# Attention of the first image: value products in four column tiles, softmax sums on VectorE

## The chip, the cores and the metric

The kernel runs on one core of one Trainium2 chip. A core has five engines with queues of their own: TensorE (PE in the profile, its weight loads PEld), VectorE (DVE), ScalarE (ACT), GpSimd (POOL) and the engine SP, which here only starts DMAs. SBUF is the working memory and PSUM the memory that TensorE writes its products to. Each has 128 partitions, and PSUM has eight banks of 512 float32 columns. All data here is float32. The metric is the time of one launch on the device in microseconds (us), lower is better.

## The reference, cut to what matters

The program is four layers on a tensor of 4 images with 384 channels and 64 x 64 positions. The change touches the attention of layer 0 alone, which for one image (batch index b) computes, with N = 4096 positions:

```python
q, k, v = qkv[:, :16], qkv[:, 16:32], qkv[:, 32:]       # 16, 16 and 96 channels, N positions
attn = softmax(einsum('bcn,bcm->bnm', q, k) * 0.25, axis=-1)
out  = einsum('bcn,bmn->bcm', v, attn)                   # 96 channels, N positions
xm   = relu(concatenate([out, x_skip], axis=1))          # 384 channels again
y    = bn(einsum('oc,bchw->bohw', w_proj, xm))
x    = x + y
```

Each output position is a mean of the 96-channel values over all 4096 positions, weighted by exponentials of scores and divided by the sum of these exponentials. The other three layers (a Fourier filter with a 3 x 3 convolution and a gate, a large block with two depthwise convolutions, a 7 x 7 convolution) come after it and are not touched.

## The kernel before, in words

`phase_a` runs layer 0 and layer 1. Its loop over the four images pairs two streams of work in `side_by_side`: `attention(b, ...)`, and `others(b, ...)`, which is the input statistics (`x_norm`) and the queries, keys and values (`qkv`) of image b+1 and layer 1 of image b-1. For b = 0 there is no earlier image, so `others` has only `x_norm(1)` and `qkv(1)`. `side_by_side` takes pieces of `others` at an even pace over the 64 steps of the attention.

A step of `attention` is a pair (i, c): query block i of 512 positions, and key chunk c of 512 positions, eight of each. Three things belong to a step:

- Scores (`scores`, L772): four matmuls, one to each quarter of 32 partitions of the array, each with 32 rows of contraction (16 channels and padding). They fill the four-bank PSUM tile `sc_s`, of which there is one (`p4`, bufs=1). Keys lie on the partitions of the result, queries on its columns.
- Exponentials (L780): ScalarE reads `sc_s` in two halves of 1024 columns and writes the SBUF tile `probs`, 2048 columns, of which there are two.
- Values times probabilities (L809): four matmuls of 128 keys each, N = 512, accumulated over the 32 matmuls of a query block into one PSUM bank `av`. The stationary operand `vt[:, 4c+v, :]` has 128 columns: 96 value channels, and 32 columns of ones. Partitions 96 to 127 of `av` therefore end up with 32 copies of the softmax sum.

A float32 matmul appears in the trace as two passes, each with a weight load of its own. So a step has 8 passes of scores and 8 passes of values.

The scores of step n+1 are written ahead of the values of step n in the program, and under `tc.high_priority()`. The Tile framework turns the program into one fixed queue for each engine before the launch: it takes instructions by priority (earlier in the program first, unless raised) as its model finds them ready, and places the semaphore waits. Each queue then runs in order on the chip.

When a query block is complete, `finish` inverts the sums (L792, 32 x 512 on VectorE) and writes `xm` as max(av, 0) times the inverse in three pieces of 32 partitions (L795). `layer0_end` follows over the next steps: it loads the input block `x_res`, normalises the other 288 channels (L831, L835), multiplies by the projection (L842: three groups of three matmuls, `proj_m`), adds the residual (L849), takes statistics (L621) and stores the block to `xa` from GpSimd's queue (L852).

PSUM in this phase: four banks for `sc_s`, two banks with the tag "a" (`pa`, `av` takes one for a query block, so one is always spare), two banks with the tag "m" (`pm`), which all other products share: `proj_m`, `ln_s`, `ln_v`, `qk_m`, `v_m`.

Of the kernel before, what the change touches and what calls it, by code (L numbers as in the profile page):

```python
# [9 lines left out]

# [1 line left out]

# [1 line left out]

# [5 lines left out]
F32 = mybir.dt.float32  # L22
AF = mybir.ActivationFunctionType
ALU = mybir.AluOpType
# [4 lines left out]
NJ = 3  # L29
P = 128  # L30
PD = 96
# [7 lines left out]
TAPS = (2, 2, 2, 2, 2, 2, 4, 4)  # L39

UNITS = C // 32

_CONST_COLS = {}
_VEC_COLS = {}
# [230 lines left out]
class _Builder:  # L275
    def __init__(self, ctx, tc, ins, out):
# [16 lines left out]

        self.tok = self.dram.tile([UNITS, B, 32, N], F32, tag="tok", name="tok")

# [13 lines left out]
        self.d53 = [  # L309
            [self.dram.tile([32, B, 32, P], F32, tag=f"d{i}{u}", name=f"d_{i}_{u}") for u in range(UNITS)]  # L310
            for i in range(2)
# [128 lines left out]
    def qkv_weights(self, pool):  # L440

        nc = self.nc
        w = self.wk("wq_raw", "lx", 2)[:, 0:PD]
        nc.scalar.dma_start(w, self.ins["w_qkv"])
        inv, shift = self.bn_scale_shift(
            "bn1", self.vec("bn1_m"), self.vec("bn1_v"), self.vec("bn1_g"), self.vec("bn1_b")
        )
        nc.vector.tensor_scalar(w, w, inv, None, ALU.mult)  # L450
        pt = self.pm("wq_pt")
        nc.tensor.transpose(pt[0:PD, 0:P], w, self.ident)
        wt = self.wk("wq_t", "ln", 3)[0 : PD + 1, 0:P]
        raw = self.wk("wq_rawt", "lx", 2)[0:PD, 0:P]
        nc.vector.tensor_copy(raw, pt[0:PD, 0:P])
        nc.vector.tensor_scalar(wt[0:PD, :], raw, self.vec("ln_w", PD), None, ALU.mult)
        pb = self.pm("wq_pb")
        nc.tensor.matmul(pb[0:1, 0:P], lhsT=self.vec("ln_b", PD), rhs=raw, start=True, stop=False)
        nc.tensor.matmul(pb[0:1, 0:P], lhsT=shift, rhs=self.ident, start=False, stop=True)
        nc.scalar.copy(wt[PD : PD + 1, :], pb[0:1, 0:P])  # L460

        self.wq4 = pool.tile([PD + 1, 4, 32], F32, tag="wq4", name="wq4")
        self.wk4 = pool.tile([PD + 1, 4, 32], F32, tag="wk4", name="wk4")
        self.wv = pool.tile([PD + 1, P], F32, tag="wv", name="wv")
        for t in (self.wq4, self.wk4, self.wv):
            nc.gpsimd.memset(t, 0.0)
        nc.gpsimd.memset(self.wk4[PD : PD + 1, :, 0:1], 1.0)
        nc.gpsimd.memset(self.wv[PD : PD + 1, PD:], 1.0)
        for g in range(4):
            nc.vector.tensor_copy(self.wq4[:, g, 1:17], wt[:, 0:16])  # L470
            nc.vector.tensor_copy(self.wk4[:, g, 1:17], wt[:, 16:32])
        nc.vector.tensor_copy(self.wv[:, 0:PD], wt[:, 32:P])
        self.wqk = pool.tile([PD + 1, 4, 32], F32, tag="wqk", name="wqk")
        nc.vector.tensor_copy(self.wqk[:, 0:3], self.wq4[:, 0:3])
        nc.vector.tensor_copy(self.wqk[:, 3], self.wk4[:, 3])
        self.score_bound(pool, wt)
# [283 lines left out]
    def attention(self, b, q, k4, vt):  # L760

        tc, nc = self.tc, self.nc

        def scores(i, c):
            p = self.probs.tile([P, 2048], F32, tag="p", name="probs")
            s = self.p4("sc_s")

            with tc.high_priority():  # L770
                for g in range(4):
                    nc.tensor.matmul(  # L772
                        s[:, g],
                        lhsT=k4[32 * g : 32 * g + 32, c],
                        rhs=q[i][32 * g : 32 * g + 32],
                        start=True,
                        stop=True,
                    )
            for h in range(2):
                nc.scalar.activation(  # L780
                    p[:, h * 1024 : (h + 1) * 1024],
                    s[:, 2 * h : 2 * h + 2].rearrange("p a b -> p (a b)"),
                    AF.Exp,
                    scale=0.25,
                )
            return p

        def finish(av):

            xm = self.work.tile([P, NJ, 512], F32, tag="xm", name="xm", bufs=1)  # L790
            rd = self.wk("av_rd", "rd", 1)
            nc.vector.reciprocal(rd[PD:P], av[PD:P])  # L792
            for g in range(3):
                at = slice(32 * g, 32 * g + 32)
                nc.vector.scalar_tensor_tensor(xm[at, 0], av[at], 0.0, rd[PD:P], ALU.max, ALU.mult)  # L795
            return xm

        st = self.stats_tile("xa_st")
        steps = [(i, c) for i in range(8) for c in range(8)]
        ahead = scores(*steps[0])  # L800
        done, end = None, iter(())
        for n_step, (i, c) in enumerate(steps):
            p = ahead
            if n_step + 1 < len(steps):
                ahead = scores(*steps[n_step + 1])
            if c == 0:
                av = self.pa("av")
            for v in range(4):
                nc.tensor.matmul(  # L809
                    av,  # L810
                    lhsT=vt[:, 4 * c + v, :],
                    rhs=p[:, v * 512 : (v + 1) * 512],
                    start=c == 0 and v == 0,
                    stop=c == 7 and v == 3,
                )
            next(end, None)
            if c == 1 and done is not None:
                end = self.layer0_end(b, i - 1, finish(done), st)
            if c == 7:
                done = av  # L820
            yield
        for _ in self.layer0_end(b, 7, finish(done), st):
            pass
        self.norm1 = self.norm_of_stats(st)

# [220 lines left out]
    def phase_b(self):  # L1046
# [5 lines left out]
        with ExitStack() as ctx:  # L1052
# [17 lines left out]
            self.units(cp)  # L1070
            self.unit_x = [[] for _ in range(UNITS)]
            for u in range(UNITS):
                st = self.bt_p.tile([P, 2, 16, 6], F32, tag="st", name="st")
                strips = self.unit_strips(u + 1) if u + 1 < UNITS else iter(())
                tok = self.unit_tok(u - 1) if u else self.unit_strips(0)
# [8 lines left out]
                self.conv_norms(u, st)  # L1084
            for _ in self.unit_tok(UNITS - 1):
                pass
# [856 lines left out]
```

## Time and profile before

| | |
|---|---|
| median of three runs | 4893.77 us (4886.19 to 4898.56) |
| the profiled execution | 4883.64 us, of which the span from first to last instruction is 4881.8 us |
| instructions | 47092 |
| TensorE busy over the span | 4432.2 us (91%) |
| VectorE busy over the span | 2764.1 us (57%) |
| ScalarE busy over the span | 1988.4 us (41%) |
| GpSimd busy over the span | 728.7 us (15%) |
| attention of image 0 | from about 62 us to 495 us of the span |

The profile is of one execution. A group line names the source line, the engine, the operation, what is written and read, the shapes, the count, busy time and mean time of one instruction, and the idle time of the engine ahead of it with what ended it. The ends of matmuls are modelled, so the distance from one start to the next says more of the pace than a matmul's own duration does.

### The profile page before, as it was taken

To read this page: it belongs to the slowest core of one execution; us is meant where nothing else is said; L and a number is where in the kernel's file an instruction comes from. 1 tells how busy PE (TensorE), PEld (TensorE's weight loads), DVE (VectorE), ACT (ScalarE), POOL (GpSimd) and SP (SyncE) were. 2 spreads that over 40 slices of the span, in tenths; PEclk is the share of its full clock that TensorE was granted. 3 is DMA by queue.
4 is the path that set the end of the run, shared out by engine and by line. 5 is a ranking of instruction groups with operands and counts; after the bars stand their busy time and mean duration, and the time that the engine had idled before them with its cause. 6 is when DMAs were issued, how large, how long until landed. Compare 5 with 4: busy or idle time off the path is not lost. (4 is left out here: it accounts for less than half of the span.)

```text
span 4881.8 us, 47092 instructions
## 1 busy us (share of the span) xinstructions
PE 4432.2 (91%) x17289; PEld 2492.5 (51%) x17289; DVE 2764.1 (57%) x4506; ACT 1988.4 (41%) x2958; POOL 728.7 (15%) x593
## 2 busy tenths in 40 slices
PE   5999999999999999989978889699999997778888
PEld 2334444344443444435467878344444443667888
DVE  6322566655566455566867778555521113667898
ACT  3444344444444443436345556311133334753321
POOL 1000000000000000000034445000000001225544
PEclk9999999999999999999979999899999998788999
DMA  5211212121211111113259999766664444896776
GB/s 186 74 34 38 83 65 72 46 76 35 69 61 60 54 46 58 59 56 121 75 167 300 281 281 305 269 252 254 242 244 155 155 155 155 312 342 188 229 254 231
DMA packets 345844, 749.06 MB, mean 153 GB/s; under 512 B 22683, under 2 KB 172294, under 8 KB 336646
## 3 DMA queue, kind: packets, MB, share of 16 engines
q1 hardware_dynamic: 279864, 471.92, 31.3%
q0 software_dynamic: 32640, 151.28, 8.0%
q10 hardware_dynamic: 33102, 122.77, 6.5%
q8 instruction: 140, 2.29, 0.2%
q14 instruction: 98, 0.80, 0.1%
HBM read 443.62 MB, written 302.25 MB: 153 GB/s over the span
## 5 line engine op out<-in xcount | busy, mean ns | idle before, releaser
L809 PE MATMUL av<-probs,vt 128*128 128x512 f32 x2048 | 955.9, 603 | 0.0
L780 ACT ACTIVATE probs<-sc_s 128x1024 f32<-128x1024 f32 x512 | 497.8, 1020 | 785.4 <-PE av L809 784.7
L809 PEld LDWEIGHTS av<-probs,vt 128*128 128x128 f32 x2048 | 368.0, 191 | 468.3 <-issue 464.6
L1005 DVE SCALAR_TENSOR_TENSOR acc<-band,vecs,acc 128x512 f32<-128x512 f32 x708 | 496.5, 747 | 45.2 <-POOL band L966 40.0
L1499 PE MATMUL h_m<-f_h,cm_w_t 128*128 128x512 f32 x1152 | 497.2, 595 | 7.4 <-ACT f_h L1487 7.4
L1216 PE MATMUL conv_m<-toep,z 128*128 128x192 f32 (+1 forms) x2304 | 447.7, 356 | 17.7 <-DVE toep L1197 17.6
L1216 PEld LDWEIGHTS conv_m<-toep,z 128*128 128x128 f32 x2304 | 411.1, 198 | 40.7 <-issue 10.2
L1813 PE MATMUL conv_m<-toep,z 128*128 128x128 f32 x3072 | 395.3, 287 | 38.3 <-POOL toep L1800 19.8
L1813 PEld LDWEIGHTS conv_m<-toep,z 128*128 128x128 f32 x3072 | 380.7, 203 | 40.5 <-POOL toep L1800 20.2
L1445 PE MATMUL h_s<-e_tok,cm_w_t 128*128 128x512 f32 x768 | 363.0, 595 | 4.2 <-DVE e_tok L1430 4.2
L1499 PEld LDWEIGHTS h_m<-f_h,cm_w_t 128*128 128x128 f32 x1152 | 219.7, 191 | 284.9 <-issue 274.3
L1197 POOL TENSOR_TENSOR toep<-w,band 128x1280 f32<-128x1280 f32 x94 | 272.3, 2901 | 314.3 <-PE conv_m L1216 199.9
L1507 DVE BATCH_NORM_STATS2 h_st<-f_h 128x6 f32<-128x512 f32 x96 | 66.5, 694 | 429.6 <-ACT f_h L1506 429.6
L772 PE MATMUL sc_s<-q,k 32*128 32x512 f32 x2048 | 294.9, 645 | 10.6 <-ACT probs L780 10.1
L928 PE MATMUL t_m<-w_in_t,xb 128*128 128x384 f32 x768 | 278.4, 497 | 3.1 <-DVE coef L945 2.9
L842 PE MATMUL proj_m<-xm,w_proj_t 128*128 128x512 f32 x576 | 271.2, 610 | 6.8 <-DVE xm L795 6.8
L1452 ACT COPY e_h<-h_s 128x1024 f32<-128x1024 f32 x96 | 97.2, 1012 | 399.9 <-PE h_s L1445 399.9
L849 DVE SCALAR_TENSOR_TENSOR x_res<-proj_m,bn_c,x_res 128x512 f32<-128x512 f32 x96 | 71.9, 749 | 324.6 <-PE proj_m L842 324.4
L1445 PEld LDWEIGHTS h_s<-e_tok,cm_w_t 128*128 128x128 f32 x768 | 146.6, 191 | 188.6 <-issue 183.3
L1454 DVE BATCH_NORM_STATS2 h_st<-e_h 128x6 f32<-128x512 f32 x192 | 123.4, 685 | 206.6 <-ACT e_h L1452 206.5
L928 PEld LDWEIGHTS t_m<-w_in_t,xb 128*128 128x128 f32 x768 | 142.5, 191 | 140.2 <-issue 59.8
L1445 PE MATMUL h_s<-z,cm_w_t 128*128 128x512 f32 x384 | 196.0, 592 | 0.0
(390 smaller groups left out, 5974.1 us busy)
## 6 DMA issues: line engine op xcount, KB each, us to landing
d<-d_o ACTq DMA_DIRECT2D x96, 512.0 KB
c_d<-d SPq DMA_DIRECT2D x96, 512.0 KB
hid<-e_h ACTq DMA_DIRECT2D x16, 3072.0 KB
f_h<-hid SPq DMA_DIRECT2D x16, 3072.0 KB
x_in<-in_x SPq DMA_DIRECT2D x96, 256.0 KB
x_res<-in_x SPq DMA_DIRECT2D x32, 768.0 KB
xa<-x_res POOLq DMA_DIRECT2D x32, 768.0 KB, 3.9
xa_in<-xa SPq DMA_DIRECT2D x32, 768.0 KB
```

The lines of the kernel that those rows point to most:

```text
L772: nc.tensor.matmul(s[:, g], lhsT=k4[32 * g : 32 * g + 32, c], rhs=q[i][32 * g : 32 * g + 32], start=True, stop=True,)
L780: nc.scalar.activation(p[:, h * 1024 : (h + 1) * 1024], s[:, 2 * h : 2 * h + 2].rearrange("p a b -> p (a b)"), AF.Exp, scale=0.25,)
L809: nc.tensor.matmul(av, lhsT=vt[:, 4 * c + v, :], rhs=p[:, v * 512 : (v + 1) * 512], start=c == 0 and v == 0, stop=c == 7 and v == 3,)
L842: nc.tensor.matmul(m, lhsT=self.w_proj[:, j, o * P : (o + 1) * P], rhs=xm[:, j], start=j == 0, stop=j == NJ - 1,)
L928: nc.tensor.matmul(m[:, 0:C], lhsT=xb[:, j], rhs=self.w_in[:, j, :], start=j == 0, stop=j == NJ - 1,)
L1005: nc.vector.scalar_tensor_tensor(out, src(j, k), w, done, ALU.mult, ALU.add)
L1197: eng.tensor_tensor(t, self.w53[:, at : at + 160].rearrange("p (m n) -> p m n", n=8).unsqueeze(2).to_broadcast([P, 20, 8, 8]), band.rearra ...
L1216: nc.tensor.matmul(m[:, c * 256 + to : c * 256 + to + 64 * (k1 - k0)], lhsT=self.z_[:, at : at + P], rhs=t[:, 10 * c + k0 : 10 * c + k1].r ...
L1445: nc.tensor.matmul(s[:, v, :], lhsT=w1[:, j, o * P : (o + 1) * P], rhs=t[j][:, v * 512 : (v + 1) * 512], start=j == 0, stop=j == NJ - 1,)
L1454: nc.vector.bn_stats(st[:, o, 8 * b + 2 * i + v, :], h[:, o, v * 512 : (v + 1) * 512])
L1499: nc.tensor.matmul(m, lhsT=w2[:, o, j * P : (j + 1) * P], rhs=h[:, o, v * 512 : (v + 1) * 512], start=o == 0, stop=o == 5,)
L1813: nc.tensor.matmul(m[:, ch * P : (ch + 1) * P], lhsT=self.z_[:, at : at + P], rhs=t[:, 8 * c + 2 * i : 8 * c + 2 * i + 2].rearrange("p m a ...
```

## The change

For image 0 alone:

- The 96 value channels are taken as three slices of 32 columns. A step's products are then twelve matmuls (three slices of channels, four key subchunks) of 128 rows and 32 columns each. The table `PLAN` puts them in three rounds of four; in a round each of the four matmuls goes to a column tile of its own (quarter g of the array's columns, which is also partitions 32g to 32g+31 of the result). There are two accumulators, `av_0` and `av_1`: an entry (k, s, v) of the plan adds slice s with subchunk v into accumulator k. The two accumulators together hold 192 of 256 partition rows, and slices 0, 1 and 2 are each split over two places.
- The ones columns are not used there. `add_up` adds the probabilities of a query block on VectorE into `acc`, 1024 columns: one addition of the two halves of `probs` at c = 0, two additions at each other c, and a last one that folds 1024 columns to 512 at c = 7.
- `evacuate` copies the two accumulators out of PSUM with two copies on ScalarE and two on VectorE, at high priority. Both banks of the tag "a" are in use in a query block, so the next block's first products wait for these copies.
- `invert`: four matmuls with a 128 x 32 tile of ones, one to each column tile, sum `acc` over the partitions and lay the 512 sums out as 128 x 128 (32 copies of 128 positions in each quarter). One reciprocal of 128 x 128 follows.
- `finish_tiles`: four matmuls with a broadcast column of the identity spread the inverse back to 96 x 512, one addition joins the two copies, and one instruction makes `xm`.
- `scores` has no raised priority there.

For the other three images the instructions are those of before.

```diff
+PLAN = (
+    ((0, 0, 3), (0, 1, 2), (0, 2, 1), (0, 0, 0)),
+    ((1, 1, 0), (0, 1, 3), (0, 2, 2), (0, 0, 1)),
+    ((1, 1, 1), (1, 2, 0), (0, 2, 3), (0, 0, 2)),
+)
...
+        self.ones = pool.tile([P, 32], F32, tag="ones", name="ones")
+        nc.gpsimd.memset(self.ones, 1.0)
...
-            with tc.high_priority():
+            with tc.high_priority() if b else nullcontext():
...
+        def products(av, c, p):
+
+            quarter = lambda g: slice(32 * g, 32 * g + 32)
+            for n, jobs in enumerate(PLAN):
+                for g, (k, s, v) in enumerate(jobs):
+                    others = [x[g] for x in PLAN[:n]], [x[g] for x in PLAN[n + 1 :]]
+                    before, behind = (any(x[:2] == (k, s) for x in o) for o in others)
+                    nc.tensor.matmul(
+                        av[k][quarter(g)],
+                        lhsT=vt[:, 4 * c + v, quarter(s)],
+                        rhs=p[:, v * 512 : (v + 1) * 512],
+                        start=c == 0 and not before,
+                        stop=c == 7 and not behind,
+                    )
+
+        def add_up(c, p):
+
+            lo, hi = p[:, 0:1024], p[:, 1024:2048]
+            if c == 0:
+                t = self.blk.tile([P, NJ, 512], F32, tag="x", name="acc_p", bufs=1)
+                self.acc = t[:, 0:2].rearrange("p a n -> p (a n)")
+                nc.vector.tensor_add(self.acc, lo, hi)
+            else:
+                nc.vector.tensor_add(self.acc, self.acc, lo)
+                nc.vector.tensor_add(self.acc, self.acc, hi)
+            if c == 7:
+                self.prob_sum = self.wk("sum_p", "acc", 5)
+                nc.vector.tensor_add(self.prob_sum, self.acc[:, 0:512], self.acc[:, 512:1024])
+
+        def evacuate(av):
+
+            a, t = self.wk("av_a", "acc", 5), self.wk("av_t", "acc", 5)
+            with tc.high_priority():
+                nc.scalar.copy(t[0:32], av[0][96:128])
+                nc.vector.tensor_copy(a[0:PD], av[0][0:PD])
+                nc.scalar.copy(t[32:64], av[1][0:32])
+                nc.vector.tensor_copy(t[64:96], av[1][32:64])
+            return a, t
+
+        def invert(total):
+
+            m = self.pm("sum_m")
+            for g in range(4):
+                nc.tensor.matmul(
+                    m[32 * g : 32 * g + 32, 0:P],
+                    lhsT=self.ones,
+                    rhs=total[:, g * P : (g + 1) * P],
+                    start=True,
+                    stop=True,
+                )
+            rd = self.sm([P, P], "av_rd")
+            nc.vector.reciprocal(rd, m[:, 0:P])
+            return rd
+
+        def finish_tiles(a, t, rd):
+
+            xm = self.work.tile([P, NJ, 512], F32, tag="xm", name="xm", bufs=1)
+            m = self.pm("rd_m")
+            for g in range(4):
+                nc.tensor.matmul(
+                    m[0:PD, g * P : (g + 1) * P],
+                    lhsT=self.ident[:, 32 * g : 32 * g + 1].to_broadcast([P, PD]),
+                    rhs=rd,
+                    start=True,
+                    stop=True,
+                )
+            nc.vector.tensor_add(t[0:PD], t[0:PD], a[0:PD])
+            nc.vector.scalar_tensor_tensor(xm[0:PD, 0], t[0:PD], 0.0, m[0:PD], ALU.max, ALU.mult)
+            return xm
...
+        close = finish if b else finish_tiles
         for n_step, (i, c) in enumerate(steps):
             p = ahead
             if n_step + 1 < len(steps):
                 ahead = scores(*steps[n_step + 1])
...
+            if b == 0:
+                if c == 0:
+                    av = self.pa("av_0"), self.pa("av_1")
+                products(av, c, p)
+                add_up(c, p)
+                if c == 0 and done is not None:
+                    done = *done, invert(self.prob_sum)
+                if c == 7:
+                    evacuated = evacuate(av)
...
             if c == 1 and done is not None:
-                end = self.layer0_end(b, i - 1, finish(done), st)
+                end = self.layer0_end(b, i - 1, close(*done), st)
...
+        if b == 0:
+            done = *done, invert(self.prob_sum)
+        for _ in self.layer0_end(b, 7, close(*done), st):
             pass
```

More of the change, by code (lines that the diff above doesn't have):

```diff
@@ L13 @@
-from contextlib import ExitStack
+from contextlib import ExitStack, nullcontext
 import numpy as np
@@ L805, in attention @@
                 ahead = scores(*steps[n_step + 1])
[L806 to L815, printed above, removed]
+            if b == 0:
[7 more added lines that the diff above has]
+                    evacuated = evacuate(av)
+            else:
+                if c == 0:
+                    av = (self.pa("av"),)
+                for v in range(4):
+                    nc.tensor.matmul(
+                        av[0],
+                        lhsT=vt[:, 4 * c + v, :],
+                        rhs=p[:, v * 512 : (v + 1) * 512],
+                        start=c == 0 and v == 0,
+                        stop=c == 7 and v == 3,
+                    )
+                evacuated = av
             next(end, None)
             if c == 1 and done is not None:
-                end = self.layer0_end(b, i - 1, finish(done), st)
+                end = self.layer0_end(b, i - 1, close(*done), st)
             if c == 7:
-                done = av
+                done = evacuated
             yield
-        for _ in self.layer0_end(b, 7, finish(done), st):
+        if b == 0:
+            done = *done, invert(self.prob_sum)
+        for _ in self.layer0_end(b, 7, close(*done), st):
             pass
```

## The prediction

> **What bounds the kernel now.** First the busy table of the stretch that the change touches, and of its inside without the start (columns: length; busy us of PE, PEld, DVE, ACT, POOL; clock; DMA).
>
> ```profile
> core 0: us, PE busy (x) PEld busy (x) DVE busy (x) ACT busy (x) POOL busy (x), PEclk, DMA share, GB/s
> 62.00:495.00 433.00, 421.84 (x1383) 169.21 (x1381) 154.42 (x245) 183.60 (x223) 11.74 (x20) 0.98 0.20 62
> 124.00:488.00 364.00, 361.81 (x1194) 143.26 (x1192) 106.56 (x157) 154.86 (x183) 8.11 (x13) 1.00 0.15 48
> ```
>
> TensorE has no holes (361.8 of 364 us), VectorE is free 71% of the time, ScalarE 57%. Matmul ends are modelled, so I went to the timeline of one plain step to see whether TensorE is full or only waiting inside.
>
> ```profile
> 201.53 1.02 ACT L780 ACTIVATE probs<-sc_s 128x1024 f32<-128x1024 f32 x1
> 202.07 1.02 PE L809 MATMUL av<-probs,vt 128*128 128x512 f32 x2
> 203.02 0.31 PEld L772 LDWEIGHTS sc_s<-q,k 32*128 32x128 f32 x8 [0.76 <-ACT probs L780]
> 203.02 1.14 PE L772 MATMUL sc_s<-q,k 32*128 32x512 f32 x8
> ...
> 204.09 3.70 PE L809 MATMUL av<-probs,vt 128*128 128x512 f32 x8
> ...
> 205.06 0.19 PEld L809 LDWEIGHTS av<-probs,vt 128*128 128x128 f32 x1 [0.24 <-issue]
> 205.31 1.94 ACT L780 ACTIVATE probs<-sc_s 128x1024 f32<-128x1024 f32 x2 [2.76 <-PE av L809]
> 205.48 0.19 PEld L809 LDWEIGHTS av<-probs,vt 128*128 128x128 f32 x1 [0.24 <-issue]
> ...
> 207.72 0.31 PEld L772 LDWEIGHTS sc_s<-q,k 32*128 32x128 f32 x8 [0.76 <-ACT probs L780]
> ```
>
> A step lasts 4.70 us (203.02 to 207.72). Passes of values follow at 0.43 us (205.06, 205.48). Eight make 3.43 of the 3.63 us from 204.09 to 207.72; scores take 1.07, two passes deep, 0.86. So each change between the four-row tiling and the full array costs 0.20 us. The exponentials end at 207.25, 0.47 us ahead of the next scores: the "ACT probs" wait is only the last semaphore. 3.43 + 0.86 + 2 x 0.20 = 4.70: TensorE's own passes set the step.
>
> Last the groups of 124 to 488 us on VectorE, and from the page the price of its longest plain addition:
>
> ```profile
> L792 DVE RECIPROCAL av_rd<-av 32x512 f32<-32x512 f32 x7 | 23.5, 3363 | 36.5 <-PE av L809 36.5
> L849 DVE SCALAR_TENSOR_TENSOR x_res<-proj_m,bn_c,x_res 128x512 f32<-128x512 f32 x21 | 15.8, 751 | 117.6 <-PE proj_m L842 117.6
> L795 DVE SCALAR_TENSOR_TENSOR xm<-av,av_rd 32x512 f32<-32x512 f32 x21 | 14.4, 683 | 0.4
> ```
> ```profile
> L1800 DVE TENSOR_TENSOR toep<-wmix,band_p 128x1024 f32<-128x1024 f32 x129 | 155.5, 1213 | 28.5 <-DMA wmix<-in_mix_t 18.4 <-PE conv_m L1813 7.4 <-issue 1.3
> ```
>
> **The Trainium skill.** "TensorEngine Tiling (Array Packing)", Tiling Modes: tiles run weight loads and matmuls in parallel, and a change of the tiling mode drains the array. The trace agrees: 0.20 us a change, and four row tiles together last as long as one. "TensorE: Matmul & The Clock Gate", Part 3: three column tiles (M=32, N=512) gave 2.38 times, within 5 ns of row tiling. No run here shows column tiles at full contraction and float32; this is the largest unknown. The same page, LDWEIGHTS (loading the stationary operand): the time goes with the columns, so an estimate of a quarter of the 190 ns row plus its fixed part; a round's four loads then replace one full load. "PSUM — Partial Sum Buffer", bank collisions: column tiles may write one bank together, so the plan needs no extra waits.
>
> **The change part by part** (gain +, loss -)
>
> 1. Passes. A step has 3 rounds x 2 = 6 passes deep for 8: 2 x 0.43 x 64 = +55.0 us, if four tiles overlap. The new step is 3.83 us. Scores end 1.14 after their start, exponentials 0.1 + 1.94 later, 3.2: still 0.6 inside the step, so ScalarE does not become the bound (22.1 + 1.2 us a block for two copies of 0.58, of 51). A round issues 16 instructions in 0.86 us, 54 ns each; `v_m` (L702) runs at that pace already, 8 passes and 8 loads in 0.86.
> 2. Mode changes. Products were in the full-array mode of everything else; now other groups change it. In TensorE's order between 62 and 495 us I count 37 foreign groups (projection, layer norm, queries, values) beside a score run: one change more, and 21 inside the value passes: two more. 79 x 0.20 = -16 us. The lower bound is 37 x 0.20 = 7, if the new order puts all beside scores.
> 3. Spreading the inverse: 8 passes of 128 columns at 0.107 (L702's pace) and two changes, 1.26 x 8 blocks = -10. `invert`: two passes deep and a start, 0.3 x 8 = -2.5. The broadcast operand has no row in the trace; I take it as a plain load (bounds 0 and -3).
> 4. Handover of the accumulators. Before, a spare bank hid it; now the next block's products wait for copies of 0.58 (ScalarE) and 0.69 (VectorE) each. Scores of the next step cover 1.07 us, `av_1` is needed one round later. Uncovered 0.1 to 1.6, when an addition of 1.21 has just started; 0.45 x 7 = -3 (bounds 0, -11). Behind the waiting products stand all later scores.
> 5. VectorE. A block now costs 106.56/7 = 15.2, less 3.36 + 3 x 0.68 = 9.8; plus 15 additions x 1.21, fold 0.69, two copies 1.38, reciprocal 3.36 x 128/512 = 0.84, addition 0.69, `xm` 0.75 = 32.3 us of a block of 51, 63%. It isn't the bound. The exponentials of step n+2 now also wait for the additions of step n (two `probs` buffers), some 4 us of slack. But what TensorE waits for from VectorE (`proj_m`, `ln_s`, `v_m` out of two "m" banks, xn for `qk_m`) can stand behind one or two additions: about 6 places a block, mostly a step ahead of need; I take 0.13 us each, -6 (bounds 0, -30).
> 6. Without the priority, scores stand in program order ahead of the products: no product pass is split off behind them. Before, the exponentials started two passes after the scores (205.31), now at once. That moves slack, not passes: 0. If scores come late behind foreign work, the 0.6 us of slack is used first, and beyond it each late step costs what it is late (0.5 us in half of the steps would be -16; I expect none, since foreign groups come less than once a step and keep TensorE busy meanwhile).
> 7. End of block 7: reciprocal and three pieces, 5.4 us, were bare at 490 to 495.66; now inverse, spread and `xm` take about 3.4: +2.
>
> No DMA is added or moved; SP's and GpSimd's queues keep their issues, and the 128 x 32 memset is at the start under loads. Layers after image 0 are unchanged and start earlier by the sum.
>
> Sum: 55 - 16 - 10 - 2.5 - 3 - 6 + 2 = about 20 us. The profiled execution would go from 4883.6 to 4864. The median of the runs lies 10.1 above that execution, so 4893.8 - 20 = **4874 us**, own range 4860 to 4886. No change can be told from 0.3%, 14.7 us, either way.
>
> **Rivals.**
>
> A, slower: column tiles with 128 rows don't overlap. Twelve matmuls in turn are 24 passes for 8: 16 x 0.43 x 64 = +440, with items 2 to 7 (35) 5369 us; in pairs, 12 passes, 110 + 35, 5039. It decides early: at 0.48 us for a pass of a round my gain is gone, at 0.52 it is a loss. Against it: row tiles start within 0.02 us of each other here. For it: four streams of 128 rows are read where one was. 14%.
>
> B, no change: VectorE's lateness. If each of 6 places a block costs one half addition (0.6) and the handover its upper bound, -29 and -11 in place of -6 and -3, 31 us more: 4905, with a band of 4886 to 4915 around it. For it: its load doubles, and its queue is in order. Against: every consumer is a step behind its producer in the program. 24%, three quarters of them within 0.3%.
>
> C, more gain: foreign work falls beside scores (7 in place of 16) and VectorE is never late: 4859; with cheaper entry by short loads, 4850. 15%.
>
> The change not doing what it says, image 0's products still in full tiles: the shapes exclude it.
>
> **How the numbers follow.** Forecast 47%, of which 39 lie below 4879 and 8 within 0.3%; C 15 faster; B 18 same, 6 slower; A 14 slower. Faster 0.54, same 0.26, slower 0.20. The forecast, C down to 4845 and most of B up to 4905 hold about 80%.
>
> **What would show it.** Right: value matmuls of 128*32 with four starts within 0.1 us and rounds at 0.43 a pass; a plain step of 3.8 us; image 0's attention over at 475 rather than 495 us; VectorE about 60% busy there; the products' wait for copies under 1 us a block. Wrong: starts 0.43 apart within a round (A); TensorE idle on "DVE" releasers by tens of us (B); ScalarE waiting for additions of `acc`, which would mean that item 5's slack is gone. A clock below 1.0 in this stretch would break every pass price.

## The result and the profile after

| | before | after |
|---|---|---|
| median of the comparison runs (10 each) | 4891.45 us (4880.44 to 4905.46) | 4877.28 us (4857.23 to 4891.00) |
| ratio after to before | | 0.9976, 95% interval 0.9965 to 0.9987 |
| the profiled execution | 4883.64 us, span 4881.8 | 4868.55 us, span 4866.7 |
| first exponential of image 0 | 61.85 us | 75.20 us |
| first exponential of image 1 (step 64) | 485.5 us | 480.1 us |

The kernel became faster by 0.24%, which is 11.7 us of 4891. The interval does not reach 1, but the gain is smaller than the 0.3% that the prediction took as its bound. The forecast was 4874 us in a range of 4845 to 4905, so the total is close. The table already shows that it did not come about as the prediction has it: the exponentials of image 0 start 13 us late, and those of image 1 still start 5 us early.

First the plain step, from the timeline of the kernel after (columns: start, duration, engine, line, what, count, and the idle time ahead with its releaser):

```profile
206.06 1.14 PE L780 MATMUL sc_s<-q,k 32*128 32x512 f32 x8
...
207.13 2.78 PE L803 MATMUL av<-probs,vt 128*32 128x512 f32 x24
...
207.26 1.94 ACT L788 ACTIVATE probs<-sc_s 128x1024 f32<-128x1024 f32 x2 [0.82 <-PE sc_s L780]
...
207.58 0.13 PEld L803 LDWEIGHTS av<-probs,vt 128*32 128x32 f32 x4 [0.30 <-issue]
...
208.01 0.13 PEld L803 LDWEIGHTS av<-probs,vt 128*32 128x32 f32 x4 [0.30 <-issue]
...
209.84 1.14 PE L780 MATMUL sc_s<-q,k 32*128 32x512 f32 x8
```

The 24 passes of the products take 2.78 us, and the rounds of four weight loads follow each other at 0.43 us (207.58, 208.01). Four column tiles therefore cost what one full pass cost. The step went from 4.70 to 3.78 us (206.06 to 209.84).

Then the busy table of the same two stretches as before:

```profile
core 0: us, PE busy (x) PEld busy (x) DVE busy (x) ACT busy (x) POOL busy (x), PEclk, DMA share, GB/s
62.00:495.00 433.00, 413.20 (x2555) 136.60 (x2554) 293.15 (x391) 194.76 (x242) 11.75 (x20) 0.94 0.20 63
124.00:488.00 364.00, 345.46 (x2331) 110.48 (x2324) 246.79 (x303) 168.75 (x203) 8.11 (x13) 0.98 0.18 59
```

VectorE is now busy 247 of 364 us, ScalarE 169. TensorE's busy time between 124 and 488 us fell from 361.8 to 345.5 us, and the granted clock over the whole stretch fell from 0.98 to 0.94. The clock points at the beginning. The same columns for the first 28 us, after and then before:

```profile
62.00:90.00 28.00, 26.89 (x54) 10.55 (x53) 17.08 (x33) 10.52 (x17) 1.56 (x3) 0.61 0.28 84
```

```profile
62.00:90.00 28.00, 25.11 (x81) 10.62 (x80) 18.85 (x37) 14.72 (x22) 1.56 (x3) 0.82 0.48 147
```

There are fewer matmuls in it (54 instead of 81) and the clock is lower (0.61 instead of 0.82).

The waits of TensorE between 62 and 500 us in the kernel after (total, times, longest) name the other place:

```profile
PE av L803 <- DVE av_a L830: 8.7, 1, 8.7
PE sc_s L780 <- ACT probs L788: 7.2, 7, 2.7
PE av L803 <- DVE av_t L832: 1.6, 5, 0.3
```

The products of the second block once wait 8.7 us for the copies out of PSUM; in later blocks the same handover costs 0.3 us. Of the 7.2 us that scores wait for exponentials, 5.5 lie in steps 6 to 8 (135 to 148 us), where the exponentials themselves wait for VectorE's additions:

```profile
145.67 1.94 ACT L788 ACTIVATE probs<-sc_s 128x1024 f32<-128x1024 f32 x2 [4.95 <-DVE acc_p L820]
```

A useful measure is where each of the 64 steps starts its exponentials. All values are from the timelines, in us of the span:

| step | before | after |
|---|---|---|
| 0 | 61.8 | 75.2 |
| 12 | 161.2 | 180.1 |
| 64 (image 1 begins) | 485.5 | 480.1 |
| from 12 to 64 | 324.3 | 300.0 |

So the change wins 24.3 us over 52 steps, and up to step 12 it has lost 18.9 us, about half of which belongs to this one execution (see "What stays open"). Behind step 64 the lead grows to 8.8 us at the first residual addition of block 7 (500.24 us before, 491.40 after). The spans differ by 15.1 us; the rest of that lies in later layers whose instructions are the same, and which vary between single executions. The stage with the two depthwise convolutions alone took 570.9 us in the profiled execution before and 562.5 us after; it begins 6.7 us earlier after than before (2478.1 and 2484.8 us).

### The profile page after: what moved, and what is told of

It is laid out like the page before. It is cut to its first block, busy times and chain, and to the rows that moved or that the text cites. A ratio compares the mean times of both kernels' runs of the same rounds, so it can differ in the third digit from the quotient of the medians.

```text
span 4866.7 us, 49663 instructions
## 1 busy us (share of the span) xinstructions
PE 4413.5 (91%) x18441; PEld 2456.1 (50%) x18441; DVE 2901.2 (60%) x4642; ACT 1998.2 (41%) x2974; POOL 728.9 (15%) x594
## 5 line engine op out<-in xcount | busy, mean ns | idle before, releaser
L898 PE MATMUL av<-probs,vt 128*128 128x512 f32 x1536 | 714.9, 602 | 0.0
L898 PEld LDWEIGHTS av<-probs,vt 128*128 128x128 f32 x1536 | 275.6, 191 | 338.1 <-issue 334.4
L780 PE MATMUL sc_s<-q,k 32*128 32x512 f32 x2048 | 310.7, 644 | 19.4 <-ACT probs L788 19.1
```

The lines of the kernel that those rows point to most:

```text
L780: nc.tensor.matmul(s[:, g], lhsT=k4[32 * g : 32 * g + 32, c], rhs=q[i][32 * g : 32 * g + 32], start=True, stop=True,)
L898: nc.tensor.matmul(av[0], lhsT=vt[:, 4 * c + v, :], rhs=p[:, v * 512 : (v + 1) * 512], start=c == 0 and v == 0, stop=c == 7 and v == 3,)
```

## The experiments

In each, the kernel named is compared with the kernel before on the same chip, in five rounds. Experiments 1 to 4, 5 to 8, and 9 and 10 were three such sets on three chips, so that between sets, and with the kernel after, only the ratios to before can be compared.

### 1 and 2. Which part loses the beginning: the priority of the scores

The theory is that the dropped priority costs the beginning; the rival is that the products' handover or VectorE does. The first kernel takes the priority back everywhere, the second only for the first nine steps.

```diff
-            with tc.high_priority() if b else nullcontext():
+            with tc.high_priority():                                             # e1_prio_all
+            with tc.high_priority() if b or 8 * i + c < 9 else nullcontext():    # e2_prio_first9
```

> The changed kernel, with the scores of image 0 at raised priority again. Theory H (the head): the new kernel loses some 13 to 20 us ahead of about 170 us of the span, because scores without priority are dealt out singly between the work that makes queries, keys and values of image 0. Then the first exponentials start near 62 us instead of 75. But later scores are put into the middle of product rounds again, two mode changes more in many steps (0.2 us each): 4870 to 4890 us, no clear difference from the changed kernel. Theory V (VectorE: additions, handover copies behind other work in its queue, are what eats the gain): the head stays as late as it is, 4877 us or more.

> The changed kernel, with raised priority for the scores of the first nine steps of image 0 alone. Theory H: first exponentials near 62 us, the attention of image 0 ends 12 to 20 us earlier than in the changed kernel, 4857 to 4866 us, ratio to before about 0.994. Theory V: no gain over the changed kernel, 4877 us.

Measured: with priority everywhere 4891.19 us, ratio 1.0013 (1.0003 to 1.0023), so the whole gain is gone (4870 to 4890 was expected). With priority for nine steps 4864.24 us, ratio 0.9957 (0.9943 to 0.9971): this beats the kernel before by some 21 us. Against the kernel after it is some 9 us better (0.0019 of 4890). The two did not run side by side and their intervals overlap at the edge, so this second step is likely rather than shown; that the four versions of experiments 5 to 9 that build on it came out at 0.9961 to 0.9965 speaks for it.

The first exponential on ScalarE of the kernel with priority for nine steps, then the kernel after:

```profile
61.56 1.01 ACT L788 ACTIVATE probs<-sc_s 128x1024 f32<-128x1024 f32 x1
```

```profile
75.20 1.02 ACT L788 ACTIVATE probs<-sc_s 128x1024 f32<-128x1024 f32 x1 [0.83 <-PE sc_s L780]
```

Why it is late stands in TensorE's timeline of the kernel after:

```profile
61.61 1.12 PE L780 MATMUL sc_s<-q,k 32*128 32x512 f32 x2
62.66 1.12 PE L699 MATMUL qk_m<-ln_xn,wqk 97*128 97x512 f32 x2
...
64.61 1.12 PE L780 MATMUL sc_s<-q,k 32*128 32x512 f32 x2
...
67.87 1.64 PE L780 MATMUL sc_s<-q,k 32*128 32x512 f32 x2
...
73.09 2.07 PE L780 MATMUL sc_s<-q,k 32*128 32x512 f32 x2
```

The four score matmuls of the first step (x2 is the two passes of one) are dealt out singly over 11.5 us, among the queries, keys and values that the framework places there. Before, all eight passes stood together at 60.12 us. The last of the four also runs at half the pace: 2.07 us for what took 1.12 at 61.61. The Trainium skill, "TensorE: Matmul & The Clock Gate", Part 1, gives half the clock as the array's state after an idle window of about 3.4 us. The trace agrees on the half: the granted clock is 0.5 from 68.3 to 99.1 us, which makes the 0.61 of the row above. It does not show the idleness: TensorE's longest wait in the 15 us before was 1.11 us, and in those 31 us it waited for nothing. What kept the clock low is not shown.

That the priority is not simply good is the other half. In the kernel with priority everywhere the stretch from step 12 to 64 lasts 319.5 us, 19.5 more than the 300.0 without. A stretch of its TensorE timeline:

```profile
251.02 1.14 PE L780 MATMUL sc_s<-q,k 32*128 32x512 f32 x8
252.09 1.49 PE L803 MATMUL av<-probs,vt 128*32 128x512 f32 x11
...
255.30 0.90 PE L855 MATMUL rd_m<-av_rd,ident 128*96 128x128 f32 x6 [1.07 <-DVE av_rd L847]
256.12 1.04 PE L803 MATMUL av<-probs,vt 128*32 128x512 f32 x2
257.23 1.14 PE L780 MATMUL sc_s<-q,k 32*128 32x512 f32 x8
```

With the scores ahead of everything else the 24 product passes fall to pieces, with other work between them. Two passes of a single tile (256.12) take 1.11 us to the next start, 0.91 without the change of mode, where two rounds of four tiles take 0.86; and each border is a change of the tiling mode. I count 169 such changes in its steps 12 to 64, 149 in the kernel after and 104 in the kernel before. The 20 changes more than in the kernel after are 4.0 us of the 19.5 at 0.20 each; the waits for the inverse (`av_rd`) are 3.2 us between 180 and 480 us, where the kernel after has none. The rest, rounds with empty tiles among it, I have not split up. Step 64 comes at 491.4 us in the kernel with priority everywhere and at 464.6 with priority for nine steps, against 485.5 before: 5.9 us later and 20.9 us earlier, which is near what the two ratios say of the whole kernel (some 6 us slower, some 21 us faster).

### 3. The priority alone, in the kernel before

```diff
-            with tc.high_priority():
+            with tc.high_priority() if b else nullcontext():
```

> The kernel before, with one edit: the scores of image 0 have no raised priority. Theory H: the same head loss without any column tiles or additions, 10 to 20 us slower than before, 4902 to 4912 us. Theory V: as before, 4891 us.

Measured: 4900.5 us, ratio 1.0038 (1.0024 to 1.0053). The edit alone, without column tiles, makes the kernel slower: 0.0038 of 4887.8 us is 18.6 us, the medians lie 12.7 apart. Its first exponentials:

```profile
73.72 1.94 ACT L780 ACTIVATE probs<-sc_s 128x1024 f32<-128x1024 f32 x2 [0.83 <-PE sc_s L772]
```

They come 11.9 us after those of the kernel before. Steps 12 to 64 last 330.2 us instead of 324.3. So scores without priority help the steady part only in the kernel with column tiles, and hurt the start in both kernels. Its longest wait of TensorE matters further down:

```profile
PE gn_pv L415 <- DVE gn_d L431: 9.8, 1, 9.8
```

### 4. VectorE's additions

This kernel leaves out the two additions of each step from c = 1 on, so the sums hold the first chunk only.

```diff
-                nc.vector.tensor_add(self.acc, self.acc, lo)
-                nc.vector.tensor_add(self.acc, self.acc, hi)
+                pass
```

> The changed kernel without the additions of the chunks c = 1 to 7 in image 0 (14 of 15 big additions in each query block are left out, so the softmax sums hold the first chunk only). It takes away 112 x 1.22 = 137 us of VectorE's work in image 0. Theory H: the head is still late, and the rest gains little, 4866 to 4874 us. Theory V: most of the missing gain comes back, 4845 to 4858 us.

Measured: 4874.34 us, ratio 0.9977 (0.9965 to 0.9989), against 0.9976 for the kernel after. The steady stretch of 180 to 460 us, first the kernel after, then without the additions:

```profile
180.00:460.00 280.00, 277.06 (x1886) 89.81 (x1886) 188.55 (x218) 135.48 (x163) 7.41 (x12) 1.00 0.13 45
```

```profile
180.00:460.00 280.00, 277.06 (x1877) 90.12 (x1878) 83.03 (x130) 134.10 (x161) 7.39 (x12) 1.00 0.14 47
```

VectorE (third of the engines) drops from 188.6 to 83.0 us of 280 while TensorE's 277.06 stays where it is; steps 12 to 64 last 300.0 us in both. The additions are hidden, although they fill VectorE to 67% there. In the head the profiled execution without them is earlier, with step 12 at 169.9 instead of 180.1 us; its span ends 3.9 us earlier (4862.8 and 4866.7), and the medians show nothing of it. Where the 10 us come from is taken up under "What stays open".

### 5 to 8. The one long wait at the first handover

The kernel with priority for nine steps still has this among TensorE's waits:

```profile
PE av L803 <- DVE av_a L830: 7.0, 1, 7.0
```

If the copies' place in VectorE's queue sets it, moving them to ScalarE should win 7 us. If the statistics of image 1 set it, of which I thought that they stand ahead of the copies in that queue, spreading their pieces over more steps should. Two kernels test one of these each, one tests both, and one puts the slower pace into the kernel before as a control.

```diff
-                nc.vector.tensor_copy(a[0:PD], av[0][0:PD])
+                nc.scalar.copy(a[0:PD], av[0][0:PD])                      # e7, e8
...
-                nc.vector.tensor_copy(t[64:96], av[1][32:64])
+                nc.scalar.copy(t[64:96], av[1][32:64])                    # e7, e8
...
-            yield from self.x_norm(b + 1)
+            for piece in self.x_norm(b + 1):                              # e5, e6, e8
+                yield piece * (3.0 if b == 0 else 1.0)
...
-        per_step = ((176 if b else 0) + (42 if b + 1 < B else 0)) / 64
+        per_step = ((176 if b else 0) + ((50 if b == 0 else 42) if b + 1 < B else 0)) / 64
```

> As e2_prio_first9 (priority for the first nine steps alone), with all four copies of the accumulators on ScalarE, none in VectorE's queue. Theory Q: the first handover costs 7 to 9 us because the copy av_a stands in VectorE's queue behind input statistics of image 1 that wait for their loads. Then TensorE's wait of 7.0 us ahead of the first products of the second block is gone and the time falls by 4 to 7 us against e2_prio_first9, ratio to before about 0.9945. In the later blocks four copies on ScalarE take 2.3 us one after the other and may cost up to 0.5 us a block. Theory L: the loads of image 1 hold the stretch anyway, and the wait only moves to the statistics of image 1 (gn_pg, gn_pv): no gain, 0.9957.

> As e2_prio_first9, with the statistics of image 1 paced three times slower in image 0's steps (so TensorE meets them near step 15, not 9). Theory Q: what stands behind waiting statistics gets free, steps 9 to 12 lose their excess of about 10 us, 5 to 10 us faster than e2_prio_first9, ratio to before about 0.994. Theory L: the loads come as fast as their buffers allow, and the queries, keys and values of image 1 are now late at the end of image 0: no gain or a loss of up to 10 us.

> Both edits of e5_slow_norm and e7_act_copies on e2_prio_first9. Theory Q: the two take away the same wait, so no more than the better of them, 0.994. Theory L: 0.9957.

> The kernel before with the same slower pace of the statistics of image 1, nothing else. It lost about 5 us at steps 10 and 11. Theory Q: little to win here, since nothing of the handover stands in VectorE's queue: 0 to -5 us, 4883 to 4888 us. Theory L: no gain or a loss as in e5_slow_norm.

| kernel | median | ratio to before | step 64 at |
|---|---|---|---|
| e7, copies on ScalarE | 4870.8 us | 0.9961 (0.9945 to 0.9977) | 470.2 |
| e5, slower statistics | 4870.46 us | 0.9961 (0.9947 to 0.9975) | 470.2 |
| e8, both | 4875.26 us | 0.9962 (0.9949 to 0.9975) | 470.4 |
| e6, slower statistics in the kernel before | 4886.13 us | 0.9992 (0.9982 to 1.0003) | 479.1 |

The gain that theory Q expected (0.994 to 0.9945) did not come. None beats 0.9957 of the version that e5, e7 and e8 stand on, though the intervals overlap, and step 64 comes some 6 us later in each of the three than its 464.6. Of these, 2.2 to 4.3 us are there already at the 399th TensorE pass, up to which the order is the same in all four: in the three the clock is halved for 10.2 us from about 112 us on, in the other it is not. The control's interval holds 1. The long wait of TensorE in the copies' kernel, in the slower one and in both together:

```profile
PE gn_pv L421 <- DVE gn_d L437: 6.8, 2, 6.6
```

```profile
PE av L804 <- DVE av_t L833: 10.4, 6, 7.4
```

```profile
PE rd_m L856 <- DVE av_rd L848: 7.6, 2, 6.5
```

The wait does not go, it changes its name. With the copies out of VectorE's queue, TensorE reaches the group norm of image 1 (`gn_pv`) and waits there for VectorE instead, as theory L of that experiment had it. The kernel of experiment 3 has a wait of 9.8 us at that place too, with no handover in it at all. What stands ahead in VectorE's queue shows the timeline of the kernel after:

```profile
120.15 0.82 DVE L621 BATCH_NORM_AGGREGATE gn_mv<-x_st 128x2 f32<-128x48 f32 x3
...
151.47 0.69 DVE L639 BATCH_NORM_STATS2 x_st<-x_in 128x6 f32<-128x512 f32 x1 [0.86 <-DMA x_in<-in_x]
...
157.72 0.69 DVE L830 COPY av_a<-av 96x512 f32<-96x512 f32 x1
...
158.46 3.62 PE L803 MATMUL av<-probs,vt 128*32 128x512 f32 x10 [8.71 <-DVE av_a L830]
```

Statistics wait for their loads, and the copies, in order on the same queue, wait behind them. But these are not the statistics of image 1. Those were complete at 120.15 us, where they are joined into means. The ones below that line belong to the next image, image 2: the program writes them in the attention of image 1, and the framework placed them this early. So the slower pace of e5, e6 and e8 did not touch what stands in the way, and their result says nothing against the queue as the cause. In e5 it moved the group norm of image 1 to 193 us, while its statistics ran up to 101 us and those of image 2 from 106 to 156 us, across the handover.

### 9 and 10. The loads of image 1's statistics in larger pieces

Each load brings a whole block (three pieces of 512 columns) of image 1, with the control in the kernel before. The edit holds for image 1 alone, and so it too leaves the statistics of image 2 as they were.

```diff
+            if b == 1:
+                x = self.block("x_in", self.ins["x"][b], i, "xo", 2)
+                self.stats(st, x, i)
+                yield 0.5
+                continue
```

> As e2_prio_first9, with the input of image 1 loaded for its statistics as whole blocks (3 x 512 columns a load, two buffers of the tag xo, which image 0 leaves free) in place of single tiles of 512 (two buffers). Theory Q2: the 7 us at steps 10 and 11 come from statistics at the head of VectorE's queue that wait about 1 us each for a tile that was asked for only when the tile two before it was done; with six tiles under way TensorE's long wait at the handover goes away: 5 to 8 us faster than e2_prio_first9, ratio to before about 0.994. Theory L: the stretch is held by something else (the chain of group means), the time stays at 0.9957.

> The kernel before with the same block loads for image 1's statistics. Theory Q2: it lost about 5 us at steps 10 and 11 and gets part of it back, 4884 to 4888 us. Theory L: as before.

Measured: on the version with priority for nine steps 4868.8 us, ratio 0.9965 (0.9952 to 0.9978); in the kernel before 4886.16 us, 1.0002 (0.9993 to 1.0011). No gain from either; step 64 comes at 463.9 us in the first, 0.8 earlier than without the edit, and at 482.9 in the second. TensorE's longest wait in the first of them:

```profile
PE gn_pv L421 <- DVE gn_d L437: 7.4, 2, 7.2
```

In the first, the statistics of image 1 in whole blocks (L629) were over at 81 us. The single tiles of image 2 (L644, the branch for the other images) still stand in VectorE's queue until 140.8 us, close ahead of the additions and copies that the group norm at 145 us waits behind:

```profile
140.11 0.69 DVE L644 BATCH_NORM_STATS2 x_st<-x_in 128x6 f32<-128x512 f32 x1 [1.41 <-DMA x_in<-in_x]
```

The handover's waits are at most 0.3 us there, and the 7 us again stand at `gn_pv`. So the 7 us are not the price of the handover. What is shown: they are met where TensorE first has to wait for VectorE at that point of the program, whichever instruction that is. That the statistics of image 2 and their loads, ahead in VectorE's queue, set their length is argued from the `DMA x_in<-in_x` releasers, not shown: no version here held these statistics back, and none made the 7 us go.

## Why the prediction was right, and where it was not

The total was right: 20 us of gain forecast, some 12 measured, well within the range. By the bound of 0.3% that the prediction set itself the result counts as no change, to which it gave 26%, against 54% for faster. That the total is near is luck in part: a loss that had no price was cancelled by terms that were priced too high.

- **Item 1, the passes: right.** Rounds at 0.43 us, a plain step of 3.78 us where 3.83 was forecast. Rival A is false. The Trainium skill, "TensorE: Matmul & The Clock Gate", Part 3, gives 2.38 times for three column tiles; at full contraction in float32 four tiles here gave 24 passes in 2.78 us, and 24 single passes of 0.43 would be 10.3, so 3.7 times.
- **Item 2, mode changes: right mechanism, size too large.** In steps 12 to 64 there are 149 against 104, 45 more, or 9.0 us at 0.20 each. The forecast for that share (52 of 64 steps) was 13. Its lower bound of 37 changes is a slip: it drops the 21 other groups, which cost one change each beside scores, so 58.
- **Item 3, spread and inversion: slightly too large.** TensorE's passes in that stretch shrink by 37.8 us (300.4 to 262.6, passes times their pace) where item 1 alone gives 44.7, so these cost 6.9. The forecast's share was 10, of which some 2.6 were mode changes, here counted under item 2. A reciprocal took 950 ns against 840 worked out.
- **Item 5, VectorE: cost nothing in the steady part.** The additions took 1.22 us each as priced, and VectorE was as full as forecast (67% against "about 60%"). The lateness of 6 us that I put on it is not there: without the additions the stretch is 300.0 us as with them. Rival B is false for the steady part. In steps 6 to 8 its sign is there, ScalarE waiting for additions, with 5.5 us of TensorE's waits; without the additions these are gone, but the wait at the handover is 13.4 us instead of 8.7, and the medians show no gain.
- **Item 4, the handover: right in later blocks, wrong once.** It costs 0.3 us a block (0.45 forecast, and "under 1 us a block" as the sign), and 8.7 us at the first. The step failed by looking only at copies and additions on VectorE, not at the statistics of image 2 ahead of them. Experiments 7 and 9 show that the 7 us then stand elsewhere, so they belong to this stretch of the program rather than to the handover.
- **Item 6, the priority: the step that failed.** "That moves slack, not passes: 0." The change of order reached the beginning, where scores have no slack because nothing yet runs behind them. Alone in the kernel before it costs 0.38%; the priority put back for nine steps in the kernel after takes the ratio from 0.9976 to 0.9957. The warning in the same item ("if scores come late behind foreign work") was the right mechanism. I looked for it in the steady part, where it does not occur: there the missing priority is worth 19.5 us, since the product passes stay together.
- **Item 7, the end of block 7: right.** The lead grows from 5.4 us at step 64 to 8.8 at the first residual addition, 3.4 us for 2 forecast.

In steps 12 to 64 the terms close: 44.7 - 9.0 - 6.9 = 28.8, less 3.0 us of TensorE's waits for copies (1.6) and exponentials (1.4) between 180 and 480 us, is 25.8; measured 24.3. The attention of image 0 was over (last `xm`) at 488.4 us instead of the 475 forecast, and at 472.9 with priority for nine steps. The prediction's last sign was also there: the clock was below 1.0 in the head, and no pass of the head was priced for that.

**What stays open.** Step 12 is late by 18.9 us in the profiled execution after, by 11.5 in experiment 3 and by 8.7 without the additions. The first 28 us without the additions:

```profile
62.00:90.00 28.00, 26.85 (x70) 10.06 (x69) 19.90 (x38) 13.14 (x21) 2.08 (x4) 0.76 0.34 105
```

The order of TensorE's first 119 passes is the same as in the kernel after, yet the last of them starts at 90.4 us here and at 100.7 there. The clock is 0.5 for 13.7 us here (64.5 to 78.2) and for 30.8 us there. The 17.1 us more at half pace are an estimate of 8.6 us of these 10.3, and TensorE waits for VectorE in neither from 68 to 90 us. So about half of the 18.9 us is the clock of that one execution, and some 10 us are left as the price of the order, as in the other two. In steps 5 to 8 the additions cost the kernel after some 6 us more, most of which its shorter wait at the handover (8.7 us instead of 13.4) gives back. How often the kernel after gets so low a clock is not known, and neither is what sets it. The test that is missing for the 7 us is a kernel that holds the statistics of image 2 back until the attention of image 1.

## What to carry to other kernels

A raised priority has a price and a use that differ by stage: at the start of a pipeline the producer of the first work needs it, in the steady part it can cut another group's passes to pieces; so price an edit of the order separately for the head, the steady part and the tail. When a change takes a wait away, ask which instruction meets the same late data next: here some 7 us appeared under four names. Before an edit is taken as a test, see in the trace which instructions it moves: five kernels here slowed or regrouped the statistics of image 1, while those of image 2 stood in the queue. And a single profiled span can't rank versions that differ by 0.2%: the spans of the kernel after and of the one with priority for nine steps are 4866.7 and 4866.9 us while their ratios to before are 0.9976 and 0.9957, and the unchanged stage with the depthwise convolutions alone took from 562.5 to 576.0 us over the twelve profiled executions.

## What the runs showed of the hardware

Four column tiles of 128 rows and 32 columns overlap as fully as four row tiles do: 0.43 us for a round of four passes, with weight loads of about 110 ns each that run beside one another. At the start the granted clock fell to 0.5 for 31 us although TensorE waited for nothing, and two passes took 2.07 us for what elsewhere took 1.12. With TensorE's passes in the same order, two executions were granted 0.61 and 0.76 over the same 28 us, so the order alone does not set it. VectorE 67% instead of 30% busy in the steady part did not move TensorE by 0.1 us in 280.
